# Windowed attention in a four-layer network: queries and keys packed to 128 rows, read-outs moved between engines, and a new order of work

## The chip, the cores and the metric

One core of a Trainium2 chip runs the whole network in one launch. The metric is the device time in microseconds of that launch. The engines are named as in the profile: PE is TensorE (PEld its weight loads), DVE VectorE, ACT ScalarE, POOL GpSimd, SP SyncE, which here only issues DMAs.

## The reference

Eight images of 56 x 56 positions and 192 channels, fp32, pass four layers; each adds its output to its input after a group normalisation. Layer 0 gates a Toeplitz product along rows and columns, layer 2 is a convolution with exponential averages, layer 3 a depthwise convolution with a two-layer network. The change lies in layer 1, shifted-window attention:

```python
x = (x - mu) * jax.lax.rsqrt(var + EPS) * gamma + beta
sx = jnp.roll(x, shift=(-3, -3), axis=(1, 2))
win = ...                                    # windows of 7 x 7 = 49 positions, 64 an image
qkv = (win @ w_qkv + b_qkv).reshape(-1, N, 3, HEADS, hd)   # 6 heads of 32
attn = softmax(q * hd**-0.5 @ k^T + bias + mask)
out = attn @ v                               # heads joined to 192 channels
out = out @ w_proj + b_proj                  # then the windows are put back
```

## The kernel before

**Layout.** An image lies as 128 x 3 x 28 x 56: the upper half of the rows on partitions 0 to 63, the lower half on 64 to 127, in three blocks j of 64 channels. Layer 1 treats an image in four groups g of seven rows; a group has eight windows in each half s, 392 positions a half. `xr` holds the normalised windows, padded.

**Layer 1's pieces.** For a group, `layer1_scores` makes
- Q (`project`, L880): four calls, two for the queries and two for the keys, each of 96 rows (three heads). Each adds up six matmuls (three blocks j, two halves s; the profile shows two records for each fp32 matmul). ScalarE reads queries out with their bias (L886), ScalarE and VectorE the keys (L888, L890);
- V (`values`, L898): two calls of two window pairs, read out by ScalarE (L905) and VectorE (L907);
- E (`scores`, L916): 48 small matmuls, then on VectorE the sum with bias and mask (L922) and the maximum (L924), on POOL the subtraction (L925);
- X (`exponents`, ScalarE, L929) and Y (`shares`: VectorE sum and reciprocal, POOL product, L934 to L936).

`layer1_mix` makes for the group whose scores are ready
- T (`turn`, L957): four transposes of the softmax to `et`, six calls, read out alternately by ScalarE (L962) and VectorE (L964);
- P (`mix`, L971): 48 matmuls of 49 x 32 with `et`, once for each half, read out to `oa` (L982, L984);
- R (`project`, L990): output projection, one call for each block j, added to the image by VectorE in two pieces (L998);
- G (`statistics`, L1001): bn_stats of the group before.

**Order.** Layer 1's engines TensorE, ScalarE, VectorE and POOL work in the order of the program. A list gives it for each group: in the turn of group g it makes the softmax and output of g and the products and scores of g + 1.

```python
plan = "X Q Y V X G Q Y N T T T N Q N P N G V N N T T T N G N N P N Q N R N E N R G E N R".split()
```

N is a filling: the next step of `layer1_norm` of the next image (a generator). Its steps are window copies on POOL (L800, two a step), squares on ScalarE (L807), twice the statistics on TensorE (L838, L842), then a square root on ScalarE (L815), a reciprocal on VectorE (L817) and four times a product `rstd` on TensorE (L822) with its use on VectorE (L827). Before the fourth group all remaining steps are run.

**PSUM.** Eight banks: three for the scores `S`, three buffers tagged `mm`, which Q, V, R and the normalisation take in turn, and two tagged `et`, which T and P take in turn. A product waits until the buffer it takes has been read out.

**Layer 0's second half** (`layer0_mix`, L470 and on) begins near 757 us. It copies the operands `lc` on POOL and `rc` on ScalarE or VectorE, and issues the loads of the gate weights `w_p` and `w_o` on POOL's queue. Its tiles take over memory of the first half, and layer 1's that of layer 0; a tile's first writer waits for the last user of what lay there.

Of the kernel before, what the change touches and what calls it, by code (L numbers as in the profile page):

```python
# [19 lines left out]
HC = 96  # L20
TT = 392
# [50 lines left out]
    ("g1", 3), ("be1", 3), ("bq", 2), ("bv", 2), ("bpr", 3),  # L72
# [18 lines left out]
def kernel(ctx: ExitStack, tc: tile.TileContext, a: dict, out: bass.AP):  # L91
# [492 lines left out]
    def layer0_mix(pool, raws, psum, ops, loaded):  # L584
# [63 lines left out]
        n, gate, first, side, xn = 0, iter(()), iter(()), iter(()), None  # L648
        os = [pool.tile([64 + W, 128, H], F32, name=f"o{k}", bufs=1) for k in range(2)]
        w_p, w_o = (resident(n, nc.gpsimd, pool) for n in ("w_p", "w_o"))  # L650
# [48 lines left out]
    def layer1_weights(pool, psum):  # L699


        w_qkv = resident("w_qkv", nc.gpsimd, pool)
        w_proj = resident("w_proj", nc.gpsimd, pool)
        ones2 = pool.tile([128, 128], F32, name="ones2", bufs=1)
        nc.gpsimd.memset(ones2, 0.0)
        for s in range(2):
            nc.gpsimd.memset(ones2[64 * s:64 * s + 64, 64 * s:64 * s + 64], 1.0 / C)
        yield
        bv = pool.tile([HC, 2], F32, name="bv", bufs=1)
        for which, t in ((0, bq), (2, bv)):  # L710
            ps = psum.tile([128, 2, 512], F32, name="bias", tag="qv")[:, 0]
            for m in range(2):
                c0 = which * C + HC * m
                for j in range(3):
                    nc.tensor.matmul(
                        ps[0:HC, m:m + 1], w_qkv[0:64, j, c0:c0 + HC], vec("be1", j, 64), start=(j == 0), stop=(j == 2)
                    )
            o = VOFF["bq" if which == 0 else "bv"]
            nc.vector.tensor_tensor(t, ps[0:HC, 0:2], vecs[0:HC, o:o + 2], ALU.add)
        nc.vector.tensor_scalar(bq, bq, HD ** -0.5, None, ALU.mult)  # L720
        yield
        ps = psum.tile([128, 2, 512], F32, name="bias", tag="qv")[:, 0]
        for s in range(2):
            for j in range(3):
                for m in range(2):
                    nc.tensor.matmul(
                        ps[64 * s:64 * s + 64, j:j + 1], w_proj[:, m, 64 * j:64 * j + 64], bv[:, m:m + 1],
                        start=(m == 0), stop=(m == 1),
                    )
        o = VOFF["bpr"]  # L730
        nc.vector.tensor_tensor(bpr, ps[:, 0:3], vecs[:, o:o + 3], ALU.add)
        for j in range(3):
            nc.vector.tensor_scalar(w_qkv[:, j], w_qkv[:, j], vec("g1", j), None, ALU.mult)
        nc.vector.tensor_scalar(w_qkv[:, :, 0:C], w_qkv[:, :, 0:C], HD ** -0.5, None, ALU.mult)
        for which in range(3):
            yield
            cs = slice(which * C, (which + 1) * C)
            ps = psum.tile([128, 2, 512], F32, name="wmean", tag="qv")[:, 0, 0:C]
            for j in range(3):
                nc.tensor.matmul(ps, ones2, w_qkv[:, j, cs], start=(j == 0), stop=(j == 2))  # L740
            nc.vector.tensor_tensor(
                w_qkv[:, :, cs], w_qkv[:, :, cs], ps.unsqueeze(1).to_broadcast([128, 3, C]), ALU.subtract
            )
        nc.gpsimd.dma_start(wgd, w_qkv)
# [25 lines left out]
    def layer1_norm(b, x, pool, psum, consts, first=False):  # L770
# [41 lines left out]
        def finish(rows):  # L812
            nc.vector.tensor_scalar(rs[rows], rs[rows], 0.0, 1e-5, ALU.max, ALU.add)
            yield
            nc.scalar.activation(rs[rows], rs[rows], AF.Sqrt)  # L815
            yield
            nc.vector.reciprocal(rs[rows], rs[rows])  # L817
            yield

# [9 lines left out]
        for g0, n in ((0, 1), (1, 1), (2, 2)) if first else ((0, 2), (2, 2)):  # L829
            sqs = []  # L830
            for g in range(g0, g0 + n):
                yield from windows(g)
                sqs.append(pool.tile([128, 2, 3, 4 * WN], F32, name="sq", bufs=2))
                yield from squares(g, sqs[-1])
# [32 lines left out]
    def layer1_scores(g, xr, pool, psum, S, es, consts):  # L867
# [3 lines left out]
        qk = [pool.tile([HC, 2, 2, TT], F32, name=f"qk{s}", bufs=1) for s in range(2)]  # L871
# [3 lines left out]
        def project(which, m):  # L875
            ps = [psum.tile([128, 512], F32, name="qk_ps", tag="mm", bufs=3)[0:HC, 0:TT] for s in range(2)]
            c0 = which * C + m * HC
            for j in range(3):
                for s in range(2):
                    nc.tensor.matmul(  # L880
                        in_pairs(ps[s]), wg[64 * s:64 * s + 64, j, c0:c0 + HC],
                        in_slots(xr[64 * s:64 * s + 64], (3 * g + j) * GW), start=(j == 0), stop=(j == 2),
                    )
            for s in range(2):
                if which == 0:
                    nc.scalar.activation(qk[s][:, 0, m], ps[s], AF.Identity, bias=bq[:, m:m + 1])  # L886
                elif s == 0:
                    nc.scalar.copy(qk[s][:, 1, m], ps[s])  # L888
                else:
                    nc.vector.tensor_copy(qk[s][:, 1, m], ps[s])  # L890

        def values(k0):
            ps = [psum.tile([128, 512], F32, name="v_ps", tag="mm", bufs=3)[:, 0:2 * C] for s in range(2)]
            for k in range(2):
                for j in range(3):
                    for s in range(2):
                        t0 = (3 * g + j) * GW + PW * (k0 + k)
                        nc.tensor.matmul(  # L898
                            ps[s][:, C * k:C * k + C], xr[64 * s:64 * s + 64, t0:t0 + 128],
                            wg[64 * s:64 * s + 64, j, 2 * C:3 * C], start=(j == 0), stop=(j == 2),  # L900
                        )
            for s in range(2):
                dst = v[s][:, k0:k0 + 2].rearrange("p w c -> p (w c)")
                if s == 0:
                    nc.scalar.copy(dst, ps[s])  # L905
                else:
                    nc.vector.tensor_copy(dst, ps[s])  # L907

        mxs = [None, None]

        def scores(s):
            bm = pool.tile([128, 24, WN], F32, name="bm")
            nc.sync.dma_start(bm.rearrange("p a b -> p (a b)"), bmask[4 * s + g])
            for y, hh, r, p, z in np.ndindex(2, 2, 3, 2, 2):
                at = WN * (2 * (2 * y + p) + z)
                nc.tensor.matmul(  # L916
                    S[64 * p:64 * p + WN, 8 * r + 4 * hh + 2 * y + z, 0:WN],
                    qk[s][32 * r:32 * r + 32, 0, hh, at:at + WN], qk[s][32 * r:32 * r + 32, 1, hh, at:at + WN],
# [12 lines left out]
        def shares(s):  # L931
# [8 lines left out]
            Q=[lambda which=which, m=m: project(which, m) for which in range(2) for m in range(2)],  # L940
            V=[lambda k0=k0: values(k0) for k0 in (0, 2)], E=each(scores),
        ), dict(X=each(exponents), Y=each(shares))

    def layer1_mix(g, x, v, pool, psum, es, consts, st):
# [4 lines left out]
        oa = [pool.tile([HC, 2, TT], F32, name=f"oa{s}", bufs=1) for s in range(2)]  # L949
# [16 lines left out]
        def mix(s):  # L966
            et = ets[s]
            po = [psum.tile([128, 512], F32, name="po", tag="et", bufs=2)[0:HC, 0:TT] for _ in range(2)]
            for y, p, hh, r, z in np.ndindex(2, 2, 2, 3, 2):
                k = 2 * y + p  # L970
                nc.tensor.matmul(  # L971
                    po[z][32 * r:32 * r + 32, 4 * WN * hh + WN * k:4 * WN * hh + WN * k + WN],
                    v[s][64 * z:64 * z + WN, k, HC * hh + HD * r:HC * hh + HD * r + HD],
# [4 lines left out]
            for z in range(2):  # L978
                dst = oa[s][:, :, 4 * WN * z:4 * WN * (z + 1)]
                src = po[z].rearrange("p (m n) -> p m n", m=2)  # L980
                if z == 0:
                    nc.scalar.copy(dst, src)  # L982
                else:
                    nc.vector.tensor_copy(dst, src)  # L984

        def project(j):
            ps = psum.tile([128, 512], F32, name="pr", tag="mm", bufs=3)[:, 0:TT]
            for m in range(2):
                for s in range(2):
                    nc.tensor.matmul(  # L990
                        ps[64 * s:64 * s + 64].rearrange("p (i w j) -> p i w j", i=7, j=7),
                        w_proj[:, m, 64 * j:64 * j + 64],
                        oa[s][:, m].rearrange("p (w i j) -> p i w j", i=7, j=7), start=(m == 0), stop=(m == 1),
                    )
            rows = ps.rearrange("p (i w) -> p i w", w=W)
            for w0, w1, c0 in ((0, 53, 3), (53, 56, 0)):
                xs = x[:, j, 7 * g:7 * g + 7, c0:c0 + w1 - w0]
                nc.vector.scalar_tensor_tensor(xs, rows[:, :, w0:w1], bpr[:, j:j + 1], xs, ALU.add, ALU.add)  # L998
# [390 lines left out]
    bq, bpr = (const.tile([p, n], F32, name=z) for p, n, z in ((HC, 2, "bq"), (128, 3, "bpr")))  # L1389
# [76 lines left out]
    with ExitStack() as st:  # L1466
# [27 lines left out]
        for kind in "QVQVQQEE":  # L1494
# [6 lines left out]
        plan = "X Q Y V X G Q Y N T T T N Q N P N G V N N T T T N G N N P N Q N R N E N R G E N R".split()  # L1501
# [161 lines left out]
def _lay_out(inp):  # L1663
# [11 lines left out]
    def both(v):  # L1675
# [4 lines left out]
    l1 = lambda n: f["L1_conv_" + n]  # L1680
    l2 = lambda n: f["L2_conv_" + n]
# [5 lines left out]
        "bq": cols(l1("b_qkv")[0:C], HC, 2), "bv": cols(l1("b_qkv")[2 * C:], HC, 2), "bpr": both(l1("b_proj")),  # L1687
# [22 lines left out]
    for r in range(2):  # L1710
# [10 lines left out]
    halves = lambda w: w.reshape(2, HC, -1).transpose(1, 0, 2)  # L1721
# [22 lines left out]
        "w_qkv": twice(l1("w_qkv")), "w_proj": halves(l1("w_proj")), "sel": sel,  # L1744
# [23 lines left out]
```

## Time and profile before

| | us |
|---|---|
| median of three runs (lowest, highest) | 5586.38 (5574.53, 5587.5) |
| the profiled execution, its own time | 5579.16 |
| its span in the profile | 5577.4 |
| layer 0, first half, from the start to about | 757 |
| layer 0, second half, until about | 1937 |
| layer 1, steady from 2030, until about | 3022 |
| PE busy over the span | 5068.6 (91%) |
| DVE, ACT, POOL busy | 3034.1, 2289.7, 1878.7 |

A line of the timeline gives the start, the time that a run of equal instructions took, engine, source line, operation, out<-in, their number, and in brackets the idle time of the engine before it and what ended it. A line of the groups gives the count, busy time and mean ns of one, and the idle time before. "issue" is idle time for which the profile shows no wait.

### The profile page before, as it was taken

Reading aid. Unit: us, or ns where it says so; the run is one execution under the profiler, and the core shown is the slowest. Engines: PE = TensorE matmul, PEld = TensorE weight load, DVE = VectorE, ACT = ScalarE, POOL = GpSimd, SP = SyncE. Lnnn points to the kernel's source line nnn. Section 1 sums busy time; section 2 is a strip of 40 time slices with the busy share of each in tenths; the row PEclk is TensorE's granted clock in tenths of the full one; section 3 lists DMA queues with packets and bytes.
Section 4 is the critical chain, followed back from the end, with each engine's and each line's share of the span. In section 5 each row is a group of like instructions: output and inputs, shape, how many; then the busy total and the mean of one; then the engine's idle time right before and its main releaser. Section 6 shows DMA issues by size and latency. Waiting matters only on the chain. (4 is left out here: it accounts for less than half of the span.)

```text
span 5577.4 us, 112511 instructions
## 1 busy us (share of the span) xinstructions
PE 5068.6 (91%) x49038; PEld 3354.8 (60%) x49038; DVE 3034.1 (54%) x4087; ACT 2289.7 (41%) x3052; POOL 1878.7 (34%) x1583
## 2 busy tenths in 40 slices
PE   7999969999999889999997989999788787999999
PEld 6788856666666545555554757776344586444444
DVE  4555534555555455655665868888777313333331
ACT  3444445555555333333332015545476402333333
POOL 5555555555555333433432014333111101101000
PEclk9999989999999989999998989999899898999999
DMA  5998996777777512322314856776687596212211
GB/s 150 240 232 225 222 301 247 274 272 274 274 272 274 166 44 72 82 74 72 84 54 101 286 216 218 241 231 200 163 232 217 218 345 263 68 59 82 78 40 27
DMA packets 533281, 1002.69 MB, mean 180 GB/s; under 512 B 256104, under 2 KB 467780, under 8 KB 501412
## 3 DMA queue, kind: packets, MB, share of 16 engines
q1 hardware_dynamic: 519984, 945.57, 52.9%
q0 software_dynamic: 8560, 40.64, 2.2%
q10 hardware_dynamic: 4244, 9.27, 0.6%
q8 instruction: 386, 6.32, 0.5%
q14 instruction: 107, 0.88, 0.0%
HBM read 665.12 MB, written 346.75 MB: 181 GB/s over the span
## 5 line engine op out<-in xcount | busy, mean ns | idle before, releaser
L462 POOL COPY lc<-lt 128x896 f32<-128x896 f32 (+1 forms) x320 | 617.0, 1937 | 491.5 <-PE op L470 485.8
L429 PE MATMUL qv<-w_qv_sb,x 64*112 64x256 f32 (+1 forms) x5376 | 685.5, 408 | 16.1 <-DVE act L435 12.3
L429 PEld LDWEIGHTS qv<-w_qv_sb,x 64*112 64x112 f32 x5376 | 594.7, 175 | 96.0 <-DVE act L435 22.6
L435 DVE TENSOR_TENSOR act<-qv,b_qv 112x640 f32<-112x640 f32 x448 | 318.6, 753 | 319.7 <-PE qv L429 230.3
L439 ACT ACTIVATE act<-act 112x640 f32<-112x640 f32 x448 | 300.4, 683 | 404.9 <-DVE act L435 394.5
L405 POOL TENSOR_TENSOR qv<-act 112x320 f32<-112x320 f32 x448 | 348.8, 805 | 277.3 <-ACT act L439 195.8
L1360 PE MATMUL ph<-y,w_sb 64*128 64x392 f32 x2304 | 397.7, 498 | 6.5 <-ACT hid L1364 6.5
L470 PE MATMUL op<-rc,lc 128*56 128x56 f32 x9216 | 351.9, 220 | 56.3 <-POOL lc L462 37.9
L470 PEld LDWEIGHTS op<-rc,lc 128*56 128x56 f32 x9216 | 327.1, 134 | 125.3 <-POOL lc L462 56.4
L1371 PE MATMUL po<-hid,w_sb 128*64 128x392 f32 x2304 | 386.3, 494 | 0.0
L1378 DVE TENSOR_TENSOR x<-x,z 128x392 f32<-128x392 f32 x96 | 71.6, 746 | 519.7 <-ACT z L1376 519.7
L880 PE MATMUL qk_ps<-xr,wg 64*96 64x392 f32 x1536 | 334.0, 537 | 1.7 <-DVE xr L827 1.7
L1091 PE MATMUL cv<-zc,wt 128*128 128x224 f32 x1536 | 312.9, 355 | 24.1 <-DMA zc<-pd 24.1
L1091 PEld LDWEIGHTS cv<-zc,wt 128*128 128x128 f32 x1536 | 290.4, 189 | 67.5 <-issue 51.4
L925 POOL TENSOR_TENSOR e<-e,mx 128x1176 f32<-128x1176 f32 x64 | 140.0, 2188 | 565.9 <-DVE mx L924 523.1
L1360 PEld LDWEIGHTS ph<-y,w_sb 64*128 64x128 f32 x2304 | 220.0, 188 | 176.0 <-issue 25.6
L503 PE MATMUL y<-pp,w_o_sb 128*64 128x392 f32 x1536 | 309.1, 499 | 6.4 <-DVE pp L497 6.4
L1106 POOL TENSOR_TENSOR rows<-rows,loc 128x896 f32<-128x896 f32 x96 | 220.5, 2297 | 274.0 <-ACT rows L1102 209.2
L480 PE MATMUL pj<-xn,w_p_sb 64*128 64x392 f32 x1536 | 289.3, 509 | 20.8 <-ACT pp L487 18.6
L1371 PEld LDWEIGHTS po<-hid,w_sb 128*64 128x64 f32 x2304 | 162.6, 137 | 213.8 <-issue 213.8
L462 ACT COPY rc<-rt 128x896 f32<-128x896 f32 (+1 forms) x160 | 280.9, 1755 | 19.5 <-DMA rt<-right 19.5
L497 DVE TENSOR_TENSOR pp<-pp,ot 128x784 f32<-128x784 f32 x128 | 124.1, 969 | 293.6 <-PE ot L492 235.0
(242 smaller groups left out, 9034.0 us busy)
## 6 DMA issues: line engine op xcount, KB each, us to landing
lt<-left SPq DMA_DIRECT2D x72, 1792.0 KB
rt<-right SPq DMA_DIRECT2D x72, 1792.0 KB
left<-qv SPq DMA_DIRECT2D x224, 252.0 KB
right<-qv SPq DMA_DIRECT2D x96, 504.0 KB
wt<-in_band_dram SPq DMA_DIRECT2D x23, 2048.0 KB
zc<-pd SPq DMA_DIRECT2D x187, 232.0 KB
pd<-pt SPq DMA_DIRECT2D x7, 5568.0 KB
bm<-bmask SPq DMA_DIRECT2D x64, 588.0 KB
```

Of the source, the lines that this page charges most:

```text
L405: nc.gpsimd.tensor_tensor(qv[:, s, s0:s1, k], *(acts[s][:, which, 0:n].rearrange("p (s d) -> p s d", d=64) for which in range(2)), ALU.mult,)
L429: nc.tensor.matmul(ps[s][:, which, 0:n], x[64 * s:64 * s + 64, j, bass.ts(i, 2 * W)], w_qv[64 * s:64 * s + 64, j, which, 64 * s0:64 * s1], ...
L435: nc.vector.tensor_tensor(acts[s][:, :, 0:n], ps[s][:, :, 0:n], b_qv[:, :, 64 * s0:64 * s1], ALU.add)
L439: nc.scalar.activation(acts[s][:, :, 0:n], acts[s][:, :, 0:n], AF.Silu)
L462: copy(c[:, 0:nu], raw.rearrange("p (w u d) -> p u d w", u=nu, d=64 // nu)[:, :, d0:d0 + 8])
L470: nc.tensor.matmul(op[64 * u:64 * u + W, i, :], lc[:, u, i], rc[:, u, i], start=True, stop=True)
L480: nc.tensor.matmul(ps[:, s, 0:TT], w_p[64 * s:64 * s + 64, j, 128 * c:128 * c + 128], xn[64 * s:64 * s + 64, j, bass.ts(t, TT)], start=(j ...
L503: nc.tensor.matmul(y[64 * s:64 * s + 64], w_o[:, 2 * g + u, 64 * j:64 * j + 64], pp[:, u, s], start=(u == 0), stop=(u == 1),)
L880: nc.tensor.matmul(in_pairs(ps[s]), wg[64 * s:64 * s + 64, j, c0:c0 + HC], in_slots(xr[64 * s:64 * s + 64], (3 * g + j) * GW), start=(j == ...
L1091: nc.tensor.matmul(dst, wt[:, c4 + i, 128 * q:128 * q + 128], zc[:, :, c4 + i, q:q + NPAIR], start=(q == 0), stop=(q == 1),)
L1360: nc.tensor.matmul(ps[:, s, 0:TT], w0[64 * s:64 * s + 64, j, m * 128:(m + 1) * 128], y[64 * s:64 * s + 64, j, ts], start=(j == 0), stop=(j ...
L1371: nc.tensor.matmul(ps[64 * s:64 * s + 64], w1[:, m, 64 * j:64 * j + 64], hid[:, m, s], start=(m == 0), stop=(m == 5),)
```

## The change

- The columns of the weights are put in another order (`heads`), so that queries and keys of all heads fill three products of 128 rows. `layer1_scores` makes three Q. ScalarE reads half 0 out with the bias, VectorE half 1 (the keys have their bias, too), and ScalarE then copies the heads that lie on other partitions than their partners to `moved`.
- V is made in four calls of one window pair, all read out by ScalarE.
- The mix puts head h < 4 on rows 32 h and the last two on rows of a second column block; its outer loop is r, which is the order of the turned tiles. ScalarE and VectorE read out two pieces each. R takes four heads at 128 rows and two at 64 rows, into one `mm` and one `et` buffer; VectorE adds it in three pieces.
- In `layer1_norm` both groups' window copies come before their squares, and one empty step is added. The list `plan` and the order in layer 1's start are new.
- The bias preparation in `layer1_weights` follows the new order of columns.
- In `layer0_mix`, `w_p` and `w_o` are allocated before the two tiles `o`.

```diff
@@ layer0_mix
+        w_p, w_o = (resident(n, nc.gpsimd, pool) for n in ("w_p", "w_o"))
         os = [pool.tile([64 + W, 128, H], F32, name=f"o{k}", bufs=1) for k in range(2)]
-        w_p, w_o = (resident(n, nc.gpsimd, pool) for n in ("w_p", "w_o"))
@@ layer1_norm
             nc.vector.reciprocal(rs[rows], rs[rows])
             yield
+            if not first:
+                yield
...
             for g in range(g0, g0 + n):
                 yield from windows(g)
+            for g in range(g0, g0 + n):
                 sqs.append(pool.tile([128, 2, 3, 4 * WN], F32, name="sq", bufs=2))
                 yield from squares(g, sqs[-1])
@@ layer1_scores
-        qk = [pool.tile([HC, 2, 2, TT], F32, name=f"qk{s}", bufs=1) for s in range(2)]
+        qk = pool.tile([128, 3, 2, TT], F32, name="qk", bufs=1)
+        moved = [pool.tile([96, 2, TT], F32, name=f"{z}2", bufs=1) for z in "qk"]
...
+        def project(m):
+            ps = [psum.tile([128, 512], F32, name="qk_ps", tag="mm", bufs=3)[:, 0:TT] for s in range(2)]
             for j in range(3):
                 for s in range(2):
                     nc.tensor.matmul(
-                        in_pairs(ps[s]), wg[64 * s:64 * s + 64, j, c0:c0 + HC],
+                        in_pairs(ps[s]), wg[64 * s:64 * s + 64, j, 128 * m:128 * m + 128],
                         in_slots(xr[64 * s:64 * s + 64], (3 * g + j) * GW), start=(j == 0), stop=(j == 2),
                     )
+            nc.scalar.activation(qk[:, m, 0], ps[0], AF.Identity, bias=bq[:, m:m + 1])
+            nc.vector.tensor_scalar(qk[:, m, 1], ps[1], bq[:, m:m + 1], None, ALU.add)
+            i, src, dst = ((1, slice(96, 128), slice(64, 96)), (0, slice(96, 128), slice(64, 96)), (1, slice(64, 128), slice(0, 64)))[m]
+            nc.scalar.copy(moved[i][dst], qk[src, m])
+
+        def values(k):
+            ps = [psum.tile([128, 512], F32, name="v_ps", tag="mm", bufs=3)[:, 0:C] for s in range(2)]
...
             for s in range(2):
...
+                nc.scalar.copy(v[s][:, k], ps[s])
...
-            for y, hh, r, p, z in np.ndindex(2, 2, 3, 2, 2):
+            for hh, y, r, p, z in np.ndindex(2, 2, 3, 2, 2):
                 at = WN * (2 * (2 * y + p) + z)
+                rows = slice(HD * r, HD * r + HD)
+                q = moved[0][rows, s] if hh and r == 2 else qk[rows, 2 * hh, s]
+                k = moved[1][rows, s] if hh else qk[rows, 1, s]
@@ layer1_mix
-            for y, p, hh, r, z in np.ndindex(2, 2, 2, 3, 2):
-                k = 2 * y + p
+            for r, y, p, hh, z in np.ndindex(3, 2, 2, 2, 2):
+                k, h = 2 * y + p, 3 * hh + r
+                row, col = (HD * h, 0) if h < 4 else (64 * z + HD * (h - 4), 4 * WN)
                 nc.tensor.matmul(
-                    po[z][32 * r:32 * r + 32, 4 * WN * hh + WN * k:4 * WN * hh + WN * k + WN],
+                    po[z][row:row + HD, col + WN * k:col + WN * k + WN],
...
+                copy, rows = (nc.scalar.copy, nc.vector.tensor_copy)[z], slice(64 * z, 64 * z + 64)
+                copy(oa[s][:, z], po[z][:, 0:4 * WN])
+                copy(oa[s][rows, 2], po[z][rows, 4 * WN:8 * WN])
...
+            for z, (tag, bufs) in enumerate((("mm", 3), ("et", 2))):
+                out.append(psum.tile([128, 512], F32, name=f"pr{z}", tag=tag, bufs=bufs)[:, 0:4 * WN])
                 for s in range(2):
...
+                        w_proj[:, 0, 64 * j:64 * j + 64], by_row(oa[s][:, z]), start=True, stop=False,
...
+            for z in range(2):
+                rows = slice(64 * z, 64 * z + 64)
+                for s in range(2):
...
+                        w_proj[rows, 1, 64 * j:64 * j + 64], by_row(oa[s][rows, 2]), start=False, stop=True,
...
+            for z, w0, w1, c0 in ((0, 0, 28, 3), (1, 0, 25, 31), (1, 25, 28, 0)):
@@ the main program
-        for kind in "QVQVQQEE":
+        for kind in "QVVQVVQEE":
...
-        plan = "X Q Y V X G Q Y N T T T N Q N P N G V N N T T T N G N N P N Q N R N E N R G E N R".split()
+        plan = "X Q N Y V N X G Q N Y V N V N T T T P N V N T T T P G Q N R N E N R N G E N R N".split()
```

## The prediction

> **What bounds the kernel now.** I read the table of stages first, then layer 1's costliest groups, then two timelines of one group of layer 1, then the start of layer 0's second half. Columns of the stage table: stretch, length, busy time (instructions) of PE, PEld, DVE, ACT, POOL, granted clock, DMA share, GB/s.
>
> ```profile
> 2380.00:2500.00 120.00, 109.89 (x2014) 63.37 (x2014) 73.06 (x106) 43.49 (x73) 47.27 (x49) 0.96 0.31 80
> 2422.00:2426.00 4.00, 2.42 (x88) 1.54 (x75) 1.60 (x3) 1.21 (x1) 1.29 (x1) 0.82 0.71 186
> 2426.00:2430.00 4.00, 4.00 (x14) 1.49 (x12) 3.90 (x6) 0.00 (x0) 2.07 (x1) 0.50 0.51 162
> ```
>
> Layer 1 (2030 to 3022 us) is TensorE's: 92% busy, VectorE 61%, ScalarE 36%. The last two rows show the clock at half for some 5 us.
>
> ```profile
> L880 PE MATMUL qk_ps<-xr,wg 64*96 64x392 f32 x1536 | 334.0, 537 | 1.7 <-DVE xr L827 1.7
> L990 PE MATMUL pr<-oa,w_proj_sb 96*64 96x392 f32 x768 | 167.7, 556 | 0.0
> L898 PE MATMUL v_ps<-wg,xr 64*128 64x192 f32 x1536 | 154.4, 335 | 15.2 <-DVE x L998 12.2 <-ACT qk L886 2.6
> L971 PE MATMUL po<-et,v 49*32 49x49 f32 x6144 | 78.3, 212 | 16.9 <-ACT et L962 16.9
> L888 ACT COPY qk<-qk_ps 96x392 f32<-96x392 f32 x64 | 30.9, 482 | 122.2 <-PE qk_ps L880 122.2
> ```
>
> Of L880's 1536 matmul records, each group of rows has 48, for four projections. The order in one group:
>
> ```profile
> 2388.63 1.66 PE L990 MATMUL pr<-oa,w_proj_sb 96*64 96x392 f32 x8
> 2390.22 1.37 PE L916 MATMUL S<-qk 32*49 32x49 f32 x96
> 2391.52 1.66 PE L990 MATMUL pr<-oa,w_proj_sb 96*64 96x392 f32 x8
> 2393.11 2.22 PE L880 MATMUL qk_ps<-xr,wg 64*96 64x392 f32 x12
> 2395.84 2.27 PE L898 MATMUL v_ps<-wg,xr 64*128 64x192 f32 x23 [0.51 <-DVE x L998]
> ...
> 2400.74 1.09 PE L957 MATMUL et_ps<-ident,e 128*128 128x128 f32 x8
> ...
> 2424.16 0.72 PE L916 MATMUL S<-qk 32*49 32x49 f32 x37 [1.58 <-issue]
> ```
>
> From start to start: a projection (Q) takes 2.15 us, an output projection (R) 1.59, scores (E) 1.29, mix (P) 1.02, three turns (T) 1.92. TensorE waits 0.51 before V because VectorE read the last R out late:
>
> ```profile
> 2388.74 1.38 DVE L922 TENSOR_TENSOR e<-S,bm 128x1176 f32<-128x1176 f32 x1 [0.54 <-PE S L916]
> 2390.23 1.38 DVE L924 TENSOR_REDUCE mx<-e 128x24 f32<-128x1176 f32 x1
> 2391.52 0.74 DVE L998 SCALAR_TENSOR_TENSOR x<-pr,bpr,x 128x371 f32<-128x371 f32 x2
> 2392.18 1.37 DVE L922 TENSOR_TENSOR e<-S,bm 128x1176 f32<-128x1176 f32 x1
> 2393.66 1.38 DVE L924 TENSOR_REDUCE mx<-e 128x24 f32<-128x1176 f32 x1
> 2394.95 0.74 DVE L998 SCALAR_TENSOR_TENSOR x<-pr,bpr,x 128x371 f32<-128x371 f32 x2
> ```
>
> That chain (scores, maximum, R, scores, maximum, R) is the second limit: it ends 7.1 us after the first E, and TensorE has only 6.6 us of work beside it. By the starts of L922, the four groups of a middle image take 29.3, 37.5, 34.7 and 28.05 us: 129.5. The second holds both statistics (2.11 each) and the stall of the last PE line above, in which the profile shows no wait but DMA is at 1.09 of its share from 2418 to 2422 us: I read it as instructions that come late (the page counts 386 packets of them on queue 8). With a shorter one and the half clock after it that is 37.5 - 28.05 - 4.2 = 5.2 us.
>
> **Part 1, the packed projections.** Three Q of 128 columns for four of 96. L1360 has 64x128 weights and the same 392 columns: 24 records in 4.17 us, so 12 cost about 2.1 to 2.18. Saved: 2.15 a group, 32 x 2.15 = 69 us of TensorE time, if nothing else gets in the way.
>
> **Part 2, output projection.** R's matmuls become 8 records of 196 columns at full height, in pairs, and 8 of 64x64. L546 runs 64x64 four at a time (24 records of 392 in 2.15 us). Streaming falls from 1.59 - 0.28 = 1.31 to 0.98; a second change of array shape costs between 0 and 0.28 (what follows L990 now). R: 1.16 to 1.44; I take 1.44, as every change of shape in this timeline shows a gap. VectorE reads it in three pieces: from 371 columns 599 ns and 21 columns 229 ns, 196, 175 and 21 cost 0.79 us start to start against 0.66.
>
> **Part 3, mix.** Neighbouring matmuls now use four places of the array instead of six. If places set the pace, 1.02 x 6/4 = 1.53; if issue does, 1.02. E, whose records go to each place twice running, takes 1.29 for the same 96, so I take 1.15: +0.13, 64 times, 8 us (bounds 0 and 33). The new order saves nothing: the second accumulator sits in the buffer of the third turn, and L971 already starts two records and then waits 0.47 for that copy. With P right after T in both halves that wait of 0.74 is paid twice a group instead of once.
>
> **Part 4, read-outs and order.** V in four pieces, both halves on ScalarE: 8 copies of 192 columns; from 512 columns 585 ns and 392 columns 482 ns, 0.31 each. Each Q adds a move of 784 columns, 0.85 to 0.87 by 392 columns 482 and 1176 columns 1209 ns (L929), and it waits for VectorE's half. All products share three PSUM buffers, so the second half of each product waits for a read-out three buffers back. I laid one group out from the end of its first E (time 0), each engine in program order, 0.1 us from end to next start.
> - VectorE: scores 0.1, maximum 1.6, R 2.9, the third bn_stats (moved to here, 0.48) 3.7, second scores 4.2, maximum 5.65, last R 6.95 to 7.75, Q0's half to 8.3.
> - TensorE: R, E, R, Q0 end at 6.5; V0 waits for R's buffer until 7.4, ends 8.45; Q1's second half waits for V0's copy, which queues on ScalarE behind Q0's move (8.4 to 9.25), until 9.6; Q1 ends 11.55; V1's second half waits for Q1's read-out, ends 13.3; V2 waits likewise for V1's copy behind Q1's move; turns at 14.8. Now they start at 12.1.
> - Then T, P 3.8, V3 1.1, T, P 3.8, Q2 2.2, R 1.45, E 1.3: 13.65. Now: 16.6.
> So 2.95 is saved in the second half and 2.7 lost in the first: about 28.4 a group where only attention runs. The softmax is not late: POOL's first scaling ends at about 12.6, before the turns, its second at 16.8 before 19.7, even with two window copies (0.5 each) before each. The moved fillings issue no DMA.
>
> The new fillings put each statistic between the last R and Q0, where it covers the wait for VectorE: group two becomes 28.4 + 2.1 - 0.95 = 29.6. Group three gets the other statistic, four rstd products (0.85 each, 3.4) and the square root between V0 and the exponent on ScalarE: two table loads of 1.28 and 0.53 in front of Q1's read-out, 2.45 on the path, and a gap of 3 us after which the clock falls (1.5): 29.6 + 3.4 + 2.45 + 1.5 = 37.
>
> The next image's load now waits for the bn_stats that stands just before the second E, so its 11 us of heavy DMA fall on Q and V, 24 records in 2 us, not on E with 96 in 1.3. So I let the 5.2 go.
>
> An image: 28.4 + 29.6 + 37 + 28.4 = 123.4 for 129.5. Six images load another: 6 x 6.1 = 37 saved; image 7 (122.7 now) and image 8 lose about 1 each: **35 saved**.
>
> [...] V's second half waits 0.41 for ScalarE's copies of Q at 2432 us. [...]
>
> After the gap of 1.58 at 2424 us the clock stood at 0.50. [...]
>
> **Part 5, layer 0's weights.** By the tile sizes, the first half's weights and images end at 56 KB of its pool and its products qv lie from there to 94. w_p and w_o lie at 72 to 82 now, so their load waits until the DMAs that read qv have landed; low they lie at 14 to 25, free at 754 us. The issues stay at their place on POOL.
>
> ```profile
> 782.72 0.59 POOL L110 DMA_DIRECT2D w_p_sb<-in_w_p_dram  x1 [22.07 <-DMA right<-qv]
> 785.61 3.40 PE L470 MATMUL op<-rc,lc 128*56 128x56 f32 x64 [23.17 <-POOL lc L462]
> ```
>
> Behind that issue POOL's copies lc wait, and TensorE for them: 23 us. Without it eight products move up, and then the third block's load is next, issued at 787.23 now. It can go at 782.6 behind the image load (whose place does not move), at best at 766, with DMA at 0.88. Gain 4 to 18; I take 8, near the low end as DMA is nearly full. From 840 on TensorE is 96% busy, so it passes on. At the other end xr lies on w_o, read until 1936; VectorE's statistics until 1943 cover that, else 3 us. The additional bias matmuls are a few columns each: nothing.
>
> **Sum.** The profiled run took 5579.2 (median of the three 5586.4): 5579 - 35 - 8 = **5536**.
>
> **Rivals.**
> - *The code stall stays*, moved to another E or P. For: all chunks are still fetched. Against: the burst's new place. 5536 + 6 x 5 = 5566.
> - *Slower: the clock halves at the V0-Q1 hole.* 1.6 us of idle time in 3.2, as much as before 2424. Price: 2.6 to 5 us at half speed, 1.3 to 2.5 lost, in all 32 groups: 42 to 80, 64 taken: 5600. It decides from about 1.2 idle in one window (the rstd gap of 1.18 was followed by it). Against: the present 0.78 gaps never did it.
> - *The waits do not bite*: products flow, and only TensorE's work counts: Q 6.5, V 4.1, T 3.8, P with its waits 3.8, R 4.3, E 2.6 are 25.1 a group, 4 x 25.1 + 4.2 + 3.4 + 3 = 111 an image, 18 less, seven times: 5445. For: VectorE gets 35 us of V copies off. Against: the three buffers.
>
> **How the numbers follow.** Forecast 0.5 (5500 to 5560), stall stays 0.18, slower 0.17, free flow 0.15. Within 0.3% (17 us, what a measurement here can tell) lies most of the second: 0.17; faster 0.66, slower 0.17. The range goes from beyond the middle between forecast and free flow, 5480, to the slower rival, 5600.
>
> **What would show it.** Right: L880's successor with 1152 records; PE waiting on ScalarE at V1 and V2 and at Q1; turns about 14.8 us after the first E; no wait for the w_p issue at 760. Wrong: a mix over 1.3, the half clock in every group, or turns at 12.5. The forecast falls if TensorE's idle time in front of V and Q is under 1 us a group or over 4.

## The result: slower by 0.65%, and the profile after

The changed kernel takes 5620.97 us (median of 4 runs, 5616.06 to 5628.17), the kernel before 5586.94 beside it: a ratio of 1.0065, 95% interval 1.0045 to 1.0086. The forecast of 5536 lies 85 us below, and the range ends 21 us below. The profiled executions, 5579.2 and 5628.2, lie 49 us apart, 15 more than the medians; the experiments show where that comes from.

First layer 1's costliest groups after, in the columns of the view before.

```profile
L884 PE MATMUL qk_ps<-xr,wg 64*128 64x392 f32 x1152 | 270.1, 544 | 11.0 <-ACT v L903 8.2 <-DVE xr L830 1.7
L898 PE MATMUL v_ps<-wg,xr 64*128 64x192 f32 x1536 | 206.1, 365 | 45.9 <-ACT v L903 19.1 <-DVE x L1000 11.2 <-ACT qk L888 8.3
L967 PE MATMUL po<-et,v 49*32 49x49 f32 x6144 | 102.6, 224 | 33.1 <-ACT et L957 33.1
L986 PE MATMUL pr<-oa,w_proj_sb 128*64 128x196 f32 x768 | 91.1, 354 | 0.0
L993 PE MATMUL pr<-oa,w_proj_sb 64*64 64x196 f32 x768 | 56.6, 363 | 0.0
```

The work went down as forecast: 1152 records of Q for 1536, 270 us for 334; R's two lines sum to 147.7 for 167.7. What went up is the mean of a V record (365 ns for 335) and the idle time before V: 45.9 us for 15.2, of which 27.4 end on ScalarE (L903 and L888) and 11.2 on VectorE. The shape of a V record is unchanged, and most of the longer mean is the slower clock: after's 24 V records between 2358.5 and 2382.3 us, at half clock, have a median of 524 ns, and in the run without the half clock (no root, below) the mean is 344. One group in which only attention runs:

```profile
2394.14 1.25 PE L898 MATMUL v_ps<-wg,xr 64*128 64x192 f32 x12 [0.90 <-DVE x L1000]
2396.40 1.91 PE L884 MATMUL qk_ps<-xr,wg 64*128 64x392 f32 x9 [0.35 <-ACT v L903]
...
2400.63 1.24 PE L898 MATMUL v_ps<-wg,xr 64*128 64x192 f32 x10 [0.68 <-ACT v L903]
2403.72 0.27 PE L967 MATMUL po<-et,v 49*32 49x49 f32 x2
2404.47 1.20 PE L967 MATMUL po<-et,v 49*32 49x49 f32 x94 [0.48 <-ACT et L957]
2410.57 2.25 PE L884 MATMUL qk_ps<-xr,wg 64*128 64x392 f32 x12
2412.74 0.94 PE L986 MATMUL pr<-oa,w_proj_sb 128*64 128x196 f32 x8
```

The waits stand where the layout of Part 4 put them: 0.90 before V0 for VectorE, 0.35 inside Q1 and 0.68 inside V2 for ScalarE's copies, 0.48 inside each mix. By the starts of L918 this group takes 28.67 us. A middle image:

| us | group one | two | three | four | image |
|---|---|---|---|---|---|
| before | 29.3 | 37.5 | 34.7 | 28.05 | 129.5 |
| forecast | 28.4 | 29.6 | 37 | 28.4 | 123.4 |
| after | 28.67 | 30.64 | 45.2 | 28.67 | 133.2 |

Three groups came within 1.1 us of the forecast. Group three is 8.2 off, in six images (44.0 in the first). Here it is in windows (stretch, length, busy time and instructions of PE, PEld, DVE, ACT, POOL, granted clock, DMA share, GB/s):

```profile
2345.00:2355.00 10.00, 9.59 (x78) 4.86 (x78) 7.76 (x14) 5.32 (x9) 5.18 (x3) 1.00 0.54 166
2355.00:2360.00 5.00, 3.03 (x19) 1.79 (x18) 4.48 (x4) 4.56 (x7) 1.10 (x1) 0.85 0.00 2
2360.00:2370.00 10.00, 9.32 (x122) 6.35 (x118) 3.15 (x6) 2.34 (x6) 2.18 (x1) 0.50 0.01 2
2370.00:2380.00 10.00, 9.32 (x125) 6.61 (x126) 3.81 (x6) 1.81 (x5) 0.00 (x0) 0.50 0.01 2
2380.00:2385.00 5.00, 5.00 (x26) 2.32 (x27) 2.61 (x5) 1.87 (x4) 0.00 (x0) 0.76 0.00 0
```

TensorE is 93% busy between 2360 and 2380, but at a granted clock of 0.50; with 0.85 and 0.76 in the windows of 5 beside, the clock is at half for 1.5 + 20 + 2.4 = 24 us (2358.49 to 2382.38). ScalarE's timeline at the start of that stretch, then TensorE's:

```profile
2353.39 1.28 ACT L816 ACT_TABLE_LOAD   x1
2354.69 0.53 ACT L816 ACTIVATE rs<-rs 128x392 f32<-128x392 f32 x1
2355.24 1.28 ACT L925 ACT_TABLE_LOAD   x1
2356.53 1.20 ACT L925 ACTIVATE e<-e 128x1176 f32<-128x1176 f32 x1
2357.64 0.57 ACT L888 ACTIVATE qk<-qk_ps,bq 128x392 f32<-128x392 f32 x1
```

```profile
2356.17 1.24 PE L898 MATMUL v_ps<-wg,xr 64*128 64x192 f32 x10 [0.72 <-DVE qk L889]
2358.26 0.82 PE L898 MATMUL v_ps<-wg,xr 64*128 64x192 f32 x2 [0.85 <-ACT qk L888]
2359.47 2.29 PE L898 MATMUL v_ps<-wg,xr 64*128 64x192 f32 x10 [0.40 <-ACT v L903]
2361.69 1.67 PE L825 MATMUL rstd<-rs,sel 32*128 32x392 f32 x2
2363.29 2.91 PE L952 MATMUL et_ps<-ident,e 128*128 128x128 f32 x12
...
2379.78 2.86 PE L884 MATMUL qk_ps<-xr,wg 64*128 64x392 f32 x8
```

Table load, root, table load and exponent stand on ScalarE in front of Q1's read-out. V1 waits 0.72 for VectorE's half of Q1, V2 waits 0.85 for ScalarE's late half and 0.40 for V1's copy behind it: 1.97 us in 4. In the run without the root (below) only a wait of 0.64 is left in V1 and V2. From 2358.5 on a product takes nearly twice its time: ten of V's records span 2.29 us instead of 1.24. In this group the clock rises only at 2382.38, 2.6 us after Q2's start at 2379.78.

The timelines of POOL, SP and TensorE at the start of layer 0's second half:

```profile
769.78 0.58 POOL L109 DMA_DIRECT2D w_p_sb<-in_w_p_dram  x1
793.65 0.37 SPq L588 DMA_DIRECT2D x<-in_x_dram  x1
794.07 0.52 SPq L453 DMA_DIRECT2D lt<-left  x1
812.91 3.08 PE L469 MATMUL op<-rc,lc 128*56 128x56 f32 x64 [25.87 <-ACT rc L461]
```

The weights' issue waits for nothing now (22.07 before), but TensorE's stall is back as 25.87 in front of the third block, whose load stands on SP right behind the image load.

### The profile page after: what moved, and what is told of

Read it like the earlier page. It is cut to its first block, busy times and chain, and to the rows that moved or that the text cites. A ratio compares the mean times of both kernels' runs of the same rounds, so it can differ in the third digit from the quotient of the medians.

```text
span 5626.4 us, 113687 instructions
## 1 busy us (share of the span) xinstructions
PE 5081.8 (90%) x49428; PEld 3419.4 (61%) x49428; DVE 3048.9 (54%) x4221; ACT 2373.2 (42%) x3308; POOL 1875.9 (33%) x1583
## 5 line engine op out<-in xcount | busy, mean ns | idle before, releaser
L884 PE MATMUL qk_ps<-xr,wg 64*128 64x392 f32 x1152 | 270.1, 544 | 11.0 <-ACT v L903 8.2
```

Source lines behind the costliest of these rows:

```text
L884: nc.tensor.matmul(in_pairs(ps[s]), wg[64 * s:64 * s + 64, j, 128 * m:128 * m + 128], in_slots(xr[64 * s:64 * s + 64], (3 * g + j) * GW), ...
```

## The experiments

Each run was timed beside the kernel before on the same chip; "after" is the changed kernel. The runs used several chips, on which the kernel before had medians of 5579.0 to 5586.9 us, so a difference between two of these medians is good to some 8 us; where it is small, layer 1's own times decide.

| edit | median us | ratio to before, 95% |
|---|---|---|
| after, no root | 5547.4 | 0.9943 (0.9928–0.9958) |
| after, Q2 early in group three | 5585.6 | 1.0009 (0.9999–1.0018) |
| before, weights low | 5578.3 | 0.9993 (0.9983–1.0002) |
| after, V split | 5609.5 | 1.0057 (1.0039–1.0075) |
| after, once more (one run) | 5622.7 | – |
| after, moves on GpSimd | 5532.2 | 0.9918 (0.9900–0.9935) |
| after, late root | 5531.2 | 0.9918 (0.9900–0.9935) |
| after, both | 5494.3 | 0.9849 (0.9833–0.9866) |
| both, image load later in the program | 5493.4 | 0.9839 (0.9821–0.9857) |
| both, V split | 5510.3 | 0.9875 (0.9857–0.9893) |
| before, weights low, image load later in the program | 5576.8 | 0.9990 (0.9977–1.0004) |
| before, weights low, image load on GpSimd | 5577.7 | 0.9996 (0.9982–1.0011) |

**No root.** Is it the two table loads?

```
-            nc.scalar.activation(rs[rows], rs[rows], AF.Sqrt)
+            if first:
+                nc.scalar.activation(rs[rows], rs[rows], AF.Sqrt)
+            else:
+                nc.scalar.copy(rs[rows], rs[rows])
```

> The changed kernel, but layer 1's square root for images 2 to 8 is a plain copy on ScalarE (the root is left out), so that no table is loaded between V0's copies and the second exponent. Theory 1 (the two table loads make TensorE wait, the clock falls to half, and the turns and mixes that follow cannot lift it until the next projection): group three goes from 45.2 to about 34 us, no half clock in it, 7 x 11 = 77 less than the changed kernel, about 5544. Theory 2 (group three is long because of its extra work and waits, and the half clock costs little): only the 2.45 us of loads and root go, 42.7, 17 less, about 5604.

5547.4: 74 less than after, theory 1's number within 4. Group three falls to 34.83 us in every image, the other groups of the middle images stay within 0.02. The whole of one group three as one window:

```profile
2327.60:2362.40 34.80, 31.06 (x574) 18.50 (x575) 26.22 (x40) 14.61 (x30) 8.76 (x4) 1.00 0.18 54
```

With the loads gone the clock is 1.00 throughout. Loads and root are 3.1 us of ScalarE's time, 2.45 on the path by the forecast; without them group three is 10.4 shorter.

**Q2 early.** What lifts the clock? In group three alone the dense Q2 stands before the turns.

```
+        dense = "X Q N Y V N X G Q N Y V N V Q N T T T P N N T T T P G V N R N E N R N G E N R N".split()
...
-                for kind in plan:
+                for kind in dense if g == 2 else plan:
```

> The changed kernel, but in group three alone the third projection stands before the first turns instead of behind the second mix, and the fourth V behind the second mix. The table loads and the gap stay. Theory 1 (only a dense product lifts the clock again): the clock is back some 3 us after it fell instead of 23, the stretch of turns and mixes takes about 11.5 us instead of 18.3, group three about 38.6, 7 x 6.5 = 45 less than the changed kernel, about 5576. Theory 2 (waits, not the clock): the same work in another order, 5621 within 5.

5585.6, 35 less than after, where theory 1 said 45 and theory 2 none. Group three takes 37.9 us in three of the middle images, 39.4 and 42.0 in the others: the clock falls as in after, is back some 3 us later, and in the long ones falls a second time among the turns and mixes. The same work in another order is worth 35 us, so the half clock is a large part of the loss. How much of the 35 is clock and how much other waits, this run does not part.

**V split.** The read-outs shared between the two engines.

```
-            for s in range(2):
-                nc.scalar.copy(v[s][:, k], ps[s])
+            nc.vector.tensor_copy(v[0][:, k], ps[0])
+            nc.scalar.copy(v[1][:, k], ps[1])
```

> The changed kernel, with the first half of each V read out by VectorE instead of ScalarE. Theory 1 (after the move of all V copies ScalarE's queue binds: Q1's and V's second halves wait 2.0 us a group for it): these waits go, 1.5 to 2 us a group, 50 to 65 less than the changed kernel, 5556 to 5571, and the half clock of group three stays. Theory 2 (VectorE is the second limit, its chain of scores, maximum and R makes V0 wait already): four copies of about 0.31 more on it, the waits change engine, 5621 to 5640.

5609.5, 11 less by the medians and 5 by the ratios, and neither theory's number. Groups one, two and four are 28.66, 30.63 and 28.66, as after: the waits of 0.90, 0.35 and 0.68 are still there, now for the half that ScalarE still reads; the next run tests whether the move in its queue is what makes it late. What changed is group three: 45.2 in four of the middle images and 38.1 in two. That is the cleanest price of the half clock, since both happen in one execution with the same instructions. Windows of two images of this kernel, first one of 38.1, then one of 45.2:

```profile
2350.00:2355.00 5.00, 3.96 (x20) 2.44 (x20) 3.37 (x7) 1.22 (x4) 2.18 (x1) 0.80 0.01 3
2355.00:2360.00 5.00, 4.32 (x114) 3.16 (x114) 2.49 (x5) 1.70 (x4) 0.00 (x0) 0.85 0.00 0
2360.00:2370.00 10.00, 8.51 (x148) 4.98 (x144) 6.27 (x12) 3.45 (x7) 0.00 (x0) 1.00 0.01 3
...
2602.00:2605.00 3.00, 2.54 (x12) 1.98 (x12) 2.43 (x5) 1.05 (x2) 0.78 (x1) 0.54 0.00 0
2605.00:2615.00 10.00, 8.92 (x116) 5.55 (x116) 3.48 (x7) 2.02 (x5) 1.41 (x1) 0.50 0.01 2
2615.00:2625.00 10.00, 9.33 (x126) 6.73 (x126) 4.64 (x9) 2.02 (x5) 0.00 (x0) 0.50 0.01 2
```

The clock falls in both; in the first 0.80 and 0.85 over 5 us each make 3.5 us at half, in the second it is at half for over 20. The difference in the group is 7.1 us. It was not Q2 that lifted the clock in the first. The stretch at half there held the end of two rstd products and 11 of the 12 turns' transposes, and behind it the clock was whole:

```profile
2353.04:2356.45 3.41, 3.41 (x14) 2.28 (x12) 2.13 (x3) 0.58 (x1) 1.20 (x1) 0.50 0.00 0
```

**Moves on GpSimd.** Which copy do Q1, V1 and V2 wait for?

```
-            nc.scalar.copy(moved[i][dst], qk[src, m])
+            if m == 2:
+                move(m)
...
+        def move(m):
...
+            (nc.scalar.copy if m == 2 else nc.gpsimd.tensor_copy)(moved[i][dst], qk[src, m])
...
-        plan = "X Q N Y V N X G Q N Y V N V N T T T P ..."
+        plan = "X Q N Y V N X G Q N Y V N V N M M T T T P ..."
```

> The changed kernel, with the moves of the first and second projection taken off ScalarE: GpSimd makes them, behind the third V. Theory 1 (the copy of V0, queued on ScalarE behind a move of 0.84 us that waits 1.24 for VectorE's half, is what the second halves of Q1, V1 and V2 wait for): of the 1.65 us that TensorE waits there in each group about 1.5 goes, 28.7 becomes 27.2, 32 x 1.5 = 48 less than the changed kernel, 5573, and less gap means less half clock in group three too, down to 5545. Theory 2 (VectorE's chain behind the last R sets the pace, as the wait of 0.87 before V0 says): the waits change their name only, 5615 to 5635, the upper end where GpSimd's scaling of the exponents comes late for the turns.

5532.2: 89 less than after and below theory 1's lower case. Groups one, two and four take 27.43, 29.46 and 27.43, 1.2 less for 1.5 expected. Group three takes 35.2 in five of seven images (38.1 and 41.1 in the others), although root and loads are still there. The window around the loads in one of the five, and TensorE's waits there:

```profile
2330.00:2350.00 20.00, 17.19 (x212) 10.11 (x208) 15.47 (x22) 10.52 (x20) 8.96 (x6) 1.00 0.22 64
```

```profile
2339.54 1.24 PE L902 MATMUL v_ps<-wg,xr 64*128 64x192 f32 x10 [0.72 <-DVE qk L889]
2341.71 1.45 PE L902 MATMUL v_ps<-wg,xr 64*128 64x192 f32 x12 [0.93 <-ACT qk L888]
2343.09 0.92 PE L825 MATMUL rstd<-rs,sel 32*128 32x392 f32 x2
```

The two gaps behind the loads stay (0.72 and 0.93) and the third of 0.40 has gone: 1.65 us in 4 instead of 1.97, and the clock stays whole; two rstd products take 0.92 where after had 1.67. The smaller sum alone does not explain that. In the second image, the group of 41.1, V waits the same 0.72 and 0.93 (at 2214.09 and 2216.26), and there the clock falls. Windows around the clock's fall, first in the group of 41.1, then in after:

```profile
2213.57:2216.99 3.42, 1.97 (x17) 1.68 (x19) 3.42 (x3) 3.05 (x5) 1.08 (x1) 1.00 0.00 0
2216.99:2220.40 3.41, 3.41 (x14) 1.87 (x11) 1.57 (x3) 0.64 (x2) 2.14 (x1) 0.50 0.00 0
...
2355.07:2358.49 3.42, 1.85 (x14) 1.18 (x12) 3.00 (x2) 3.36 (x5) 1.03 (x1) 1.00 0.01 2
```

Behind these 1.45 us idle in 3.42 (1.57 in after) the clock is at half; behind the same two gaps in the group of 35.2 it is not. What makes the difference is not shown, so the five groups of 35.2 do not owe their clock to the edit alone. GpSimd makes a move in 0.83 us, ScalarE in 0.84; there it is in nobody's way.

**Late root.** The fillings laid where their engines are idle: the root behind V2's copies, its reciprocal before the first mix, one rstd product before each of four mixes.

```
+        plans = [p.split() for p in (
+            "X Q N Y V N X G Q N Y V N V N T T T L P N V N T T T P G Q N R N E N R N G E N R N",
+            "X Q N Y V N X G Q N Y V N V N T T T P N V N T T T P G Q N R N E N R N G E N R N",
+            "X Q N Y V X G Q Y V V N T T T N P V T T T N N P G Q R E R G E R",
+            "X Q Y V X G Q Y V V T T T N P V T T T N P G Q R E R G E R",
+        )]
...
+            late = steps
...
-                if g == 3:
-                    run(steps)
...
-                for kind in plan:
-                    if kind == "N":
-                        next(steps, None)
+                for kind in plans[g]:
+                    if kind in "NL":
+                        next(late if kind == "L" else steps, None)
```

> The changed kernel with other fillings in groups three, four and one: the root behind V2's copies, its reciprocal before the first mix, one rstd product before each of four mixes (groups three, four, four, and one of the next image behind its turns). Theory 1 (no gap, no half clock; the 3.4 us of rstd lie partly in the 0.5 us that each mix waits): group one 29.2, two 30.6, three and four 29.5 each, 119 an image for 133, 7 x 13 = 91 less than the changed kernel, 5530. Theory 2 (rstd, its two scalings of 1.57 on VectorE and the loads cost the same wherever they stand, as waits of the turns or read-outs): 125 to 128 an image, 5565 to 5585.

5531.2, theory 1's number. The groups are 28.78, 30.63, 31.36 and 28.90: 119.7 for 133.2. ScalarE shows why the loads cost so little now:

```profile
2329.79 1.28 ACT L816 ACT_TABLE_LOAD   x1
2331.09 0.53 ACT L816 ACTIVATE rs<-rs 128x392 f32<-128x392 f32 x1
2331.52 1.05 ACT L957 COPY et<-et_ps 128x512 f32<-128x512 f32 x2
...
2342.74 1.28 ACT L925 ACT_TABLE_LOAD   x1
```

The first load and the root run beside the first turns, whose copies follow; the second load runs at the end of the group, where ScalarE has nothing else.

**Both, and both with two additions.**

> Both edits together: moves on GpSimd and the fillings with the late root. If both theories 1 hold and add up, 5530 - 48 = 5482; if the moves give nothing, 5530 as the one with the late root alone.

5494.3: theory 1's sum was 5482. The two gains, 89 and 90 us, come to 127 together, since each of them alone takes the half clock out of most or all of the group threes. The groups are 27.55, 29.46, 30.2 and 27.68, 114.9 us. The window over all middle images, and TensorE's waits in one group four:

```profile
2131.50:2821.40 689.90, 646.28 (x13299) 417.91 (x13300) 472.98 (x775) 312.12 (x618) 342.83 (x348) 1.00 0.29 83
```

```profile
2341.27 1.25 PE L902 MATMUL v_ps<-wg,xr 64*128 64x192 f32 x12 [0.90 <-DVE x L1004]
2349.04 0.66 PE L956 MATMUL et_ps<-ident,e 128*128 128x128 f32 x4 [0.24 <-ACT et L961]
```

The clock is whole in this window, and in that group 0.90 for VectorE before V0 is the only wait over a quarter of a us.

The same with V's first halves read out by VectorE:

> The kernel with moves on GpSimd and late root, and the first half of each V read out by VectorE. Theory 1 (once the moves are gone ScalarE's copies hold nothing back, TensorE waits in a group only 0.90 for VectorE before V0 and 0.24 twice for the turns' copies): 5494 within 5, groups unchanged. Theory 2 (two engines for the read-outs help or hurt): 5480 where V's halves still come late, 5505 where VectorE's four copies delay the softmax's sums.

5510.3, 16 slower, past theory 2's end. Groups one and four are each 0.36 longer (27.91 for 27.55, 28.03 for 27.67), and in group four V2 waits 0.37 for the half that ScalarE reads, where the kernel above shows no wait:

```profile
2352.03 1.24 PE L902 MATMUL v_ps<-wg,xr 64*128 64x192 f32 x10 [0.37 <-ACT v L907]
```

With the moves out of the way, ScalarE alone does better than two engines.

> Moves on GpSimd, late root and the late image load together: 5494 less what the image load gives, 5486 to 5494. Layer 1's groups as with the two edits before, 27.5, 29.5, 30.2 and 27.7 us, and no half clock in any of them between the second and the seventh image.

5493.4, no gain from the image load; the runs on the weights say why. The last part of the expectation failed: in group three of the second and the seventh image the clock was at half for 3.41 us (from 2201.80 and 2778.66), and these groups took 32.06 and 31.71 for 30.2.

**The weights.** The kernel before with this edit alone:

```
+        w_p, w_o = (resident(n, nc.gpsimd, pool) for n in ("w_p", "w_o"))
         os = [pool.tile([64 + W, 128, H], F32, name=f"o{k}", bufs=1) for k in range(2)]
-        w_p, w_o = (resident(n, nc.gpsimd, pool) for n in ("w_p", "w_o"))
```

> The kernel before, with only layer 0's two weights allocated ahead of os. Theory W1 (the wait for the weights gives way to the third block's load behind the image load, and the 9 us that the first half of layer 0 lost have nothing to do with the place): 5587 within 5, the first half's last product at 754 us, two stalls of TensorE between 785 and 820 that sum to some 33 us. W2 (the place gives what the prediction said): 5579. W3 (the low place makes the first half's stalls): 5596, last product of the first half near 763.

The ratio is 0.9993 (0.9983 to 1.0002). From the mix's first to its last product there are 1133.5 us for 1134.0 before: W1, the stall changed its name and nothing to speak of was gained. These are single profiles: over all kernels with the weights low and the image load left on SP this stretch takes 1130.9 to 1134.5, so the place gave at most some 3 us. The first half ended at 763.7 us in this profile, which looked like W3, until the next run.

> The changed kernel once more, as it is, for a second profiled execution. If the stalls of layer 0's first half belong to the program, its last product stands at 762.8 us again; if they differ from execution to execution, anywhere between 753 and 768. Group three again between 38.1 and 45.2.

The changed kernel as it is: its first half ends at 757.7, 5.1 earlier than in its other profile; group three is 45.2 again (5622.7 in this one run). Over all kernels here the first half ends between 753.6 and 767.8 whatever was edited. So 9.2 us between two profiles in that half need no part of the change: 5.1 appear between two executions of one program. That covers most of the step from 34 (medians) to 49.

Two runs went after the third block's load. The first moved the image load behind eight steps in the program:

```
-        x = [load(0)]
+        x = []
...
+                    if n == 8:
+                        x.append(load(0))
```

> The kernel before with the two weights low, and layer 0's first image for the second half loaded after eight steps instead of ahead of the first one. Theory (with the weights' wait gone, the third block's load stands on SP behind the image load, which waits until the last writes from qv have landed): the load goes some 4 us earlier, TensorE's stalls between 770 and 825 sum to some 29 us instead of 33, first to last product of the mix 1129.5 us instead of 1133.5. Rival (the third block's load waits for its buffer or for its own data, whatever stands before it): 1133.5 as before. The forecast's 8 us would be 1126.

On SP's queue the order is not the program's here: the image load went at 789.72, in front of the third block's at 790.14, as before, and 1133.1 us says nothing on the question. The second made it `load(0, nc.gpsimd)`:

> The kernel before with the two weights low, and layer 0's first image loaded from GpSimd's queue after eight steps, so that it no longer stands on SP ahead of the third block's load (the run before this left it there). Theory (SP's order held the third block back): its load goes some 3.5 us earlier, right behind the last write from qv, and first to last product of the mix falls from 1133.5 to about 1130 us. Rival (the third block's load waits for its own data or buffer): 1133.5. Time within 6 of the kernel before either way.

1130.5 us, 3 less, the theory's number; the time stays at 0.9996 (0.9982 to 1.0011). The 3 us alone do not show the theory right: the kernel with Q2 early, whose image load stands on SP as in after, has 1130.9. TensorE's stall in front of the third block does speak for it, 21.9 us where the other kernels with the weights low have 25.9 to 29.1. SP's queue then:

```profile
787.77 2.19 SPq L415 DMA_DIRECT2D right<-qv  x2
790.07 1.27 SPq L454 DMA_DIRECT2D rt<-right  x1
```

The third block's load now goes right behind the last write from qv, and what holds it is that queue of writes.

## Why the prediction was wrong

*Parts 1 to 3* held. Q 2.17 from start to start, R 0.87 + 0.52 = 1.39 for 1.44, P 1.13 for 1.15, and the mix's wait of about 0.75 twice a group.

*Part 4, the layout*, held for what it laid out: turns 15.0 us after the end of the first E for 14.8, groups of 28.67 for 28.4. The stall in group two let go, 30.64 for 29.6. From first to last scores layer 1 took 1032.1 us for 996.4, where 35 less was forecast: a miss of 71, of which these small ones are some 15.

*Group three's term failed.* It gave the half clock 1.5 us, after the short dips that the trace before shows, where a projection stands in the stretch at half (the one at 2424.6 lasts 6.83 us, not the "some 5" that were read from two windows, so it costs 3.4; the one at 2472.4 lasts 3.41). In the new order rstd, turns and mixes follow for 18 us, and the clock stayed at half for 23.9. The experiments price the parts: without the root 34.83, that is 4.2 over group two for the rstd products (3.4 forecast); with the loads but a clock that comes back after 3.4 us 38.1 (in the V split); with the clock at half to Q2 45.2. So the forecast of 37 was right to 1.1 us but for the last 7.1, in six images (5.9 in the first). With the other misses: 6 x 8.2 + 7.0 = 56, 15, and 8 for the weights turn -43 into +36, beside 34 in the medians.

*Part 5* failed: 8 taken, 0.5 measured, at most 3 in any profile, below the bound of 4. It named the next thing that would be late, the third block's load behind the image load, and still took a gain, from a load that could go at 782.6, 4.6 earlier than before. In after it went at 794.07: counted from the first half's last product (753.6 before, 762.8 after) that is 2.4 earlier, since SP's writes from qv end near 790 and the image load goes only at 793.65.

*The rivals.* The slower one had the sequence, holes between V and Q and half clock behind them, at the wrong place and for the wrong time: the V0–Q1 hole, 0.90 and 0.35 in a steady group, never did it in after. Its point of decision, about 1.2 us idle in one window, is not shown as a limit. In after 1.25 us idle between 2393.2 and 2396.6, that hole, left the clock at 1.00; before, 1.42 idle in the 3.4 us up to 2472.39, with the gap of 1.18 in front of rstd, were followed by half clock; and the gaps of 0.72 and 0.93 were followed by it in one group of the run with the moves on GpSimd and not in another. What decides stays open. The stall in the code did not stay. Free flow, 5445, fell to the waits, but 5494 with the two edits shows that much of it could be had.

*Read-outs and the clock.* V's wait of 0.41 for ScalarE's copies, at 2432 us before, pointed the right way: after packing, copies on ScalarE ended 27.4 of the 45.9 us that TensorE stood idle in front of V. Sharing the read-outs between both engines gave nothing in the steady groups (28.66 for 28.67) and cost 0.36 a group once the moves were gone (27.91 for 27.55); taking the moves, which read no PSUM, off ScalarE gave 1.2 a group (27.43).

In after, gaps of 0.72 and 0.85 us were followed by 23.9 us at 0.50; before, the gap of 1.58 at 2424 was followed by 6.83. In after V, rstd and turns then ran from 2359.47 to 2366.2 without a gap, 6.7 us, and it stayed at 0.50; it rose 2.6 us after Q2's start. That the turns keep it down is not the whole cause: in the short group of the V split the clock was whole again behind the stretch with 11 of the 12 transposes. In after all 24 of the group's transposes ran at half, and it rose only with Q2 behind them.

*Left open*: layer 1's entry, from the end of layer 0 to the first scores, took 65.5 us for 62.5; with the late root alone it was 62.5 again, and its cause is not known. Nor is it shown what parts the V split's two kinds of group: the fall came 19.6 us after the first scores in the short one and 16.6 in the long one, with the end of rstd and the turns behind it in the short one and V in the long one. What lifts the clock is open: in after 6.7 us with TensorE busy throughout did not.

## What to carry to other kernels

Before pricing a stall of TensorE, look at what follows it: in front of a projection the clock was at half for 3.4 or 6.8 us, in front of 18 us of small products, turns and waits mostly for 24, 7 us more in the group. Gaps of 0.72 and 0.93 us were followed by half clock in one group and not in another of the same execution; so take them away rather than count on a limit. When an in-order queue makes others wait, look for the instruction in it that nobody needs yet (here the moves, 0.84 us each, and the table loads, 1.28 each) and move that one, before sharing the rest among engines. And when a wait is taken away, ask what the next one waits for: TensorE's stall of 23 us behind the weights came back as 26 behind the same queue of writes.

## What the hardware showed beyond that

The half clock outlasted the gaps in front of it: in after 1.57 us of idle time (0.72 and 0.85) were followed by 23.9 us at 0.50, with TensorE busy for 22.14 of them (93%), and in one execution of the V split the same group took 38.1 or 45.2 us by that alone. After's middle images take 133.12 to 133.17 us, and in all of them the fall comes at the same place of the group (16.8 us after its first scores): these equal groups are not so many independent observations. Two executions of the same program differed by 5 us in a half of layer 0 that no edit touches.
